# Cross-attention with image prompts on one core: the last batch's sums spread over three engines, its end in chunks of channels, its order written out

## The chip, the cores and the metric

The kernel runs on one core of a Trainium2 chip. The metric is the device time of one launch in microseconds. A core has five engines that each work through their own queue in order: TensorE (PE in the profile; its weight loads are PEld), VectorE (DVE), ScalarE (ACT), GpSimd (POOL) and SyncE (SP, which here only issues DMAs). They wait for each other by semaphores. TensorE reads SBUF and writes PSUM, which here is used as eight banks of 128 x 512 float32.

## The reference

Eight batches; x is 112 x 320 per batch, the context 375 x 512, of which the last 4 rows are image-prompt tokens. There are 20 heads of 16 channels. Everything is float32.

```python
q = heads(hidden_states @ W_q)
k_t = heads(text_ehs @ W_k)
v_t = heads(text_ehs @ W_v)
probs_t = softmax(einsum('bhsd,bhtd->bhst', q, k_t) * attn_scale)
text_out = einsum('bhst,bhtd->bhsd', probs_t, v_t)
...
attn_scores = einsum('bhsd,bhnd->bhsn', q, k_ip) * attn_scale
qsem = _l2norm(einsum('bhst,bte->bhse', probs_t, text_ehs))
sem = einsum('bhse,bne->bhsn', qsem, _l2norm(ip_ehs))
fused = attn_scores + SEM_SCALE * sem
probs_ip = softmax(fused) * spatial_mask[None, None, :, None]
ip_out = einsum('bhsn,bhnd->bhsd', probs_ip, v_ip)
out = (text_out + ip_out) @ W_out + b_out + residual
```

`_l2norm` divides a vector by its length. `qsem` has 512 entries for each head and query, and only its length and its products with four prompt vectors are needed.

## The kernel before

Each batch's 20 heads are treated in five groups of four (`GROUP`, `groups`). For a group:

- `scores` (L467): TensorE multiplies q and k into a PSUM bank `ps_s` of 112 x 371, per head.
- `probabilities` (L485): VectorE takes the negative maximum `nmx` (L489), ScalarE the exponential `p` (L493), and SP sends p to the tile `xg` (L496), without normalisation.
- `transposed` (L500): VectorE transposes `xg` by 32 x 32 blocks into `xgT` (L504).
- `multiplied` (L510): TensorE multiplies p by a wide matrix `u` (L523), 12 blocks of tokens times four heads, into four banks `ps_qd` of up to 392 columns. `u` holds half of the symmetric Gram matrix of the context (so the first 371 columns, multiplied by p and summed, give the squared length of `qsem`), then the products with the prompt vectors, a column of ones (the softmax's sum) and the head's 16 value channels.
- `reduced` (L533): per head, ScalarE copies the last 21 columns to `pvs` (L536), and VectorE multiplies the first 371 columns by p and sums them into one column of `ss` (L538).
- `placed` (L441): GpSimd copies the next group's value channels into `u` (L445), in three pieces, each of which waits until TensorE has read the old ones.

When all heads of a batch are reduced, `finish` (L551) makes the output: roots and reciprocals of `ss` and of the softmax's sum `z`, a softmax over the four prompt logits (L578 to L604), the weighted prompt values `wv` (L606, L612) added to the text part `attn` (L585, L613, L614) on GpSimd or another engine, a transpose on TensorE (L620), its copy `aT` (L624), the output projection `ps_o` (L633), the addition of residual and bias `xb` (L571, L640) and the store (L643). ScalarE loads a table for the root (L579) and another for the exponential (L595).

The loop (L744) runs over batch and group. Scores and probabilities run two groups ahead (`LEAD`), the transpose one ahead. `between` (L665) places pieces of other work after each group: the next batch's Gram matrix, values, keys and context transposes, and one stage of `finish` of the batch before. In the last batch no next batch exists, so only `finish` of batch 6 is there. The last batch's own `finish` comes in two parts: 16 heads (L777, begun after group 3, with its elementwise work on GpSimd), and the last 4 (L782, on VectorE).

Six banks serve the products: four `ps_qd`, two `ps_mm` (function `bank`), and two `ps_sc` hold scores. In the last batch some of the groups' banks come from `ps_mm` (L516).

The order of TensorE, SP and VectorE is as written (L89: `manual_schedule(engines=engines)`). The instructions of ScalarE and GpSimd are ordered by a scheduler from their dependences; only the prologue is written out for all engines.

Of the kernel before, what the change touches and what calls it, by code (L numbers as in the profile page):

```python
# [20 lines left out]
def kernel(  # L21
# [511 lines left out]
    def reduced(b, g):  # L533
        s = st[b]
        for a, (h, ps) in enumerate(zip(groups[g], s.pop(("qd", g)))):
            nc.scalar.copy(s["pvs"][:, h, :], ps[:S, TT:UW])  # L536
            junk = small.tile([S, TT], F32, tag="junk", name=f"junk_{b}_{h}", bufs=1)
            nc.vector.tensor_tensor_reduce(  # L538
                out=junk,
                in0=ps[:S, :TT],  # L540
                in1=s["p", g][:, a, :],
                scale=1.0,
                scalar=0.0,
                op0=ALU.mult,
                op1=ALU.add,
                accum_out=s["ss"][:, h : h + 1],
            )
        del s["p", g]


    def finish(b, heads=(0, H), eng=None, late=False):  # L551

        s = st[b]
        eng = eng or nc.gpsimd
        h0, h1 = heads
        n = h1 - h0
        part = slice(h0, h1)

        def sm(name):
            return small.tile([S, H], F32, tag=name, name=f"{name}_{b}_{h0}", bufs=2)[:, :n]  # L560

        def sm4(name):
            return small.tile([S, H, NIP], F32, tag=name, name=f"{name}_{b}_{h0}", bufs=2)[:, :n]

        def over_ip(t):
            return t.unsqueeze(2).to_broadcast([S, n, NIP])

        pvs = s["pvs"][:, part]
        if not late:
            s["xb"] = work.tile([S, C], F32, tag="xb", name=f"xb_{b}", bufs=1)  # L570
            nc.gpsimd.tensor_tensor(s["xb"], x_sb[:, b, :], bias_sb, ALU.add)  # L571
        z = sm("z")
        nc.vector.tensor_copy(z, pvs[:, :, NIP])

        z2 = sm("z2")
        nc.vector.scalar_tensor_tensor(z2, z, EPS * EPS, z, ALU.mult, ALU.mult)
        rn = sm("rn")
        nc.vector.tensor_tensor(rn, s["ss"][:, part], z2, ALU.max)  # L578
        nc.scalar.activation(rn, rn, AF.Sqrt)  # L579
        nc.vector.reciprocal(rn, rn)  # L580
        zr = sm("zr")
        nc.vector.reciprocal(zr, z)
        attn = attn_ring[b % 2]
        ah = attn[:, :C].rearrange("p (h d) -> p h d", d=D)[:, part]
        eng.tensor_tensor(  # L585
            ah, pvs[:, :, NIP + 1 :], zr.unsqueeze(2).to_broadcast([S, n, D]), ALU.mult
        )
        fu = sm4("fu")
        nc.vector.tensor_tensor(fu, pvs[:, :, :NIP], over_ip(rn), ALU.mult)
        nc.vector.scalar_tensor_tensor(fu, fu, SEM_SCALE, s["ipl"][:, part], ALU.mult, ALU.add)  # L590
        mx = sm("mx")
        nc.vector.tensor_reduce(mx, fu, AX.X, ALU.max)
        nc.vector.tensor_tensor(fu, fu, over_ip(mx), ALU.subtract)
        ex = sm4("ex")
        nc.scalar.activation(ex, fu, AF.Exp)  # L595
        yield

        sx = sm("sx")
        nc.vector.tensor_reduce(sx, ex, AX.X, ALU.add)
        rx = sm("rx")  # L600
        nc.vector.reciprocal(rx, sx)
        nc.vector.tensor_scalar_mul(rx, rx, sm_sb)
        w = sm4("w")
        nc.vector.tensor_tensor(w, ex, over_ip(rx), ALU.mult)  # L604
        wv = work.tile([S, NIP, H, D], F32, tag="wv", name=f"wv_{b}_{h0}", bufs=1)[:, :, :n]
        eng.tensor_tensor(  # L606
            wv,
            s["vip"][:, :, part],
            w.rearrange("p h n -> p n h").unsqueeze(3).to_broadcast([S, NIP, n, D]),
            ALU.mult,  # L610
        )
        eng.tensor_tensor(wv[:, :2], wv[:, :2], wv[:, 2:], ALU.add)  # L612
        eng.tensor_tensor(ah, ah, wv[:, 0], ALU.add)  # L613
        eng.tensor_tensor(ah, ah, wv[:, 1], ALU.add)  # L614
        yield

        i0, i1 = h0 * D // P, -(-h1 * D // P)
        ps = bank(f"ps_a_{b}_{h0}")
        for i in range(i0, i1):
            nc.tensor.transpose(  # L620
                ps[:, i * S : (i + 1) * S], attn[:, i * P : (i + 1) * P], ident[:S, :S]
            )
        aT = work.tile([P, NC, S], F32, tag="aT", name=f"aT_{b}_{h0}")
        nc.scalar.copy(  # L624
            aT[:, i0:i1], ps[:, i0 * S : i1 * S].rearrange("p (i s) -> p i s", s=S)
        )
        yield

        if not late:
# [12 lines left out]

        nc.sync.dma_start(out[b], ob)  # L643
        del st[b]
        yield
# [12 lines left out]
    def run(key, make, pieces=1):  # L658

        if key not in gens:  # L660
            gens[key] = make()
        for _ in range(pieces):
            next(gens[key], None)

    def between(b, g):  # L665

        nb = b + 1
        new = nb < B
        later = [bs for bs in pairs if bs[0] == (nb if b == 0 else nb + 1)]
        if g == 0:  # L670
            if b == 0:
                run(("pp",), None)
            if new:
                run(("g", nb), lambda: gram(nb), 3)
            if b > 0:
                run(("f", b - 1), lambda: finish(b - 1))
        if g == 1:
            if new:
                run(("v", nb), lambda: values(nb), 2)
            run(("t", b), lambda: prompt_logits(b))  # L680
            if b > 0:
                run(("f", b - 1), None)
        if g == 2 and new:
            run(("v", nb), None)
            run(("k", nb), lambda: keys(nb))
        if g == 3:
            if new:
                run(("k", nb), None, 2)
            if b > 0:
                run(("f", b - 1), None)  # L690
        if g == 4:
            if nb + 1 < B:
                run(("c", nb + 1), lambda: transposed_context(nb + 1), 3)
            if b > 0:
                run(("f", b - 1), None)
        if b == 0 and g in (1, 2) or b > 0 and g == 4:
            for bs in later:
                run(("q", bs[0]), lambda: project_queries(bs), 3 if b == 0 else 6)
# [42 lines left out]
    more_constants()  # L741
    prologue.close()

    for n, (b, g) in enumerate(steps):  # L744
        coming = steps[n + LEAD] if n + LEAD < len(steps) else None
        for j, _ in enumerate(multiplied(b, g)):
            at = {0: (0, 1), 4: (2, 3)}.get(j, ())
            for a in at if coming else ():
                scores(*coming, a)
                probabilities(*coming, a)  # L750
            if j == 2 and n + 1 < len(steps):
                transposed(*steps[n + 1])
        reduced(b, g)
        if n + 1 < len(steps):
            placed(*steps[n + 1])
        new = b + 1 < B
        if g == 0 and b > 1:
            run(("f", b - 2), None)
        if new:
            if g == 1:  # L760
                gram_to_dram(b + 1)
                load_next(b + 2)
            elif g == 2:
                gram_to_groups(b + 1, (0, 1))
# [61 lines left out]
```

## Time and profile before

| | |
|---|---|
| median of 3 runs | 498.68 us (497.8 to 499.25) |
| the profiled execution | 498.01 us, span 496.2 us |
| TensorE busy | 468.3 us, 94% of the span |
| VectorE busy | 321.1 us, 65% |
| ScalarE busy | 180.1 us, 36% |
| GpSimd busy | 105.9 us, 21% |
| mean granted clock of TensorE | 0.972 |
| groups 0 to 4 of the last batch, first matmul | 437.13, 445.16, 457.16, 465.80, 471.40 us |
| end of group 4 | 477.05 us |
| last addition `ob` ends | 493.40 us |

All times in the profile are microseconds from the start of the span of one profiled execution; the span is what the engines' records cover, and the execution's own time is 1.81 us more. A line of an engine's order of time gives start, length, engine, line of the kernel, operation and tiles; in square brackets stands how long the engine was idle before it, and what ended that. The slices on the page divide the span into 40; a digit is a busy share in tenths.

### The profile page before, as it was taken

The numbers are of one execution on the slowest core, as the hardware profiler recorded it, in microseconds if no ns is written. First come the engines' busy times: TensorE is split into PE (matmuls) and PEld (weight loads), VectorE is DVE, ScalarE is ACT, GpSimd is POOL, SyncE is SP. The second block draws the span as 40 slices with busy tenths as digits, with TensorE's granted clock in tenths as the row PEclk, the third lists the DMA queues.
The fourth block names the chain that finished last, engine by engine and source line by source line (L and its number), as shares of the span: only waits on it lengthen the run. The fifth ranks groups of instructions, "written<-read, shape, count | busy, mean of one in ns | idle before, by whom it ended". The sixth has DMA issues, their size and how long they took to land.

```text
span 496.2 us, 12853 instructions
## 1 busy us (share of the span) xinstructions
PE 468.3 (94%) x5106; PEld 361.8 (73%) x5106; DVE 321.1 (65%) x692; ACT 180.1 (36%) x505; POOL 105.9 (21%) x245
## 2 busy tenths in 40 slices
PE   6999999999999999999999999999999999987963
PEld 3657777788777787788778787788777887766751
DVE  3045456687765775687756776687756776678862
ACT  2253232235334352335324342335324432243232
POOL 4301200002501124012501124012501232011540
PEclk9997999999999999999999999999999999998895
DMA  7588447542595236942595236842595227732300
GB/s 217 157 198 237 100 152 163 156 114 63 154 228 153 58 95 172 210 121 67 163 229 142 67 98 171 199 116 76 171 220 140 67 87 162 195 101 78 101 13 12
DMA packets 61075, 67.24 MB, mean 136 GB/s; under 512 B 22128, under 2 KB 56192, under 8 KB 61016
## 3 DMA queue, kind: packets, MB, share of 16 engines
q1 hardware_dynamic: 60096, 65.32, 50.3%
q10 hardware_dynamic: 920, 1.11, 0.8%
q8 instruction: 40, 0.66, 0.6%
q14 instruction: 19, 0.16, 0.1%
HBM read 31.65 MB, written 8.17 MB: 80 GB/s over the span
## 4 chain that ended last, share of the span: by engine, by line
PE 84%; DVE 5%; ACT 3%; DMA 2%; POOL 2%; issue 2%; SPq 1%; POOLq 0%; ACTq 0%; DVEq 0%
PE ps_qd L523 37%; PE ps_k L393 11%; PE ps_v L409 11%; PE ps_g L362 9%; PE ps_s L476 7%; PE ps_q L289 2%; PE ps_c L339 2%; PE ps_o L633 2%; DVE junk L538 1%; POOL wv L606 1%; DMA vr<-vd 1%; DVE qm L298 1%; PE ps_kip L237 1%; PE ps_ip L456 1%; DMA ip_sb<-in_ctx_dram 1%
## 5 line engine op out<-in xcount | busy, mean ns | idle before, releaser
L523 PE MATMUL ps_qd<-u,xgT 32*112 32x296 f32 (+11 forms) x3840 | 244.4, 365 | 3.5 <-POOL u L445 1.4
L523 PEld LDWEIGHTS ps_qd<-u,xgT 32*112 32x112 f32 x3840 | 196.8, 174 | 33.6 <-issue 7.3
L493 ACT ACTIVATE p<-ps_s,nmx 112x371 f32<-112x371 f32 x160 | 82.3, 568 | 159.8 <-DVE nmx L489 141.6
L489 DVE TENSOR_REDUCE nmx<-ps_s 112x1 f32<-112x371 f32 x160 | 77.4, 528 | 76.0 <-PE ps_s L476 74.7
L504 DVE STREAM_TRANSPOSE xgT<-xg 128x1536 f32<-128x1536 f32 x40 | 118.9, 2971 | 5.2 <-DMA xg<-p 5.2
L538 DVE CUSTOM_DVE_ANT_0 junk<-ps_qd,p 112x371 f32<-112x371 f32 x160 | 87.1, 544 | 45.3 <-ACT pvs L536 28.0
L476 PE MATMUL ps_s<-kT,qm 32*112 32x371 f32 x320 | 75.0, 496 | 2.8 <-ACT p L493 2.2
L445 POOL COPY u<-vr 128x64 f32<-128x64 f32 x120 | 26.6, 238 | 224.8 <-PE ps_qd L523 161.5
L393 PE MATMUL ps_k<-ctxT,wk_sb 128*128 128x371 f32 x192 | 63.6, 480 | 0.0
L409 PE MATMUL ps_v<-wv_sb,ctxT 128*128 128x320 f32 x192 | 55.6, 440 | 0.0
L393 PEld LDWEIGHTS ps_k<-ctxT,wk_sb 128*128 128x128 f32 x192 | 35.7, 190 | 21.7 <-issue 1.1
L476 PEld LDWEIGHTS ps_s<-kT,qm 32*112 32x112 f32 x320 | 36.8, 173 | 15.8 <-ACT kT L400 3.2
L362 PE MATMUL ps_g<-ctxT 128*128 128x375 f32 (+2 forms) x192 | 45.3, 394 | 0.7 <-issue 0.7
L409 PEld LDWEIGHTS ps_v<-wv_sb,ctxT 128*128 128x128 f32 x192 | 35.2, 190 | 13.5
L362 PEld LDWEIGHTS ps_g<-ctxT 128*128 128x128 f32 x192 | 33.4, 197 | 12.3 <-issue 3.8
L400 ACT COPY kT<-ps_k 128x371 f32<-128x371 f32 x24 | 11.3, 469 | 41.4 <-PE ps_k L393 41.3
L606 POOL TENSOR_TENSOR wv<-vip,w 112x1280 f32<-112x1280 f32 (+1 forms) x8 | 19.2, 2404 | 31.8 <-DVE w L604 31.8
L298 DVE TENSOR_SCALAR qm<-ps_q,emask 128x224 f32<-128x224 f32 (+1 forms) x25 | 9.2, 400 | 24.2 <-PE ps_q L289 24.0
L416 ACT COPY vext<-ps_v 128x320 f32<-128x320 f32 x24 | 10.2, 427 | 33.5 <-PE ps_v L409 33.5
L371 POOL TENSOR_TENSOR ug<-ug,half 128x128 f32<-128x128 f32 (+1 forms) x24 | 11.3, 472 | 41.6 <-ACT ug L370 41.6
L536 ACT COPY pvs<-ps_qd 112x21 f32<-112x21 f32 x160 | 16.5, 200 | 6.9 <-PE ps_qd L523 6.9
L289 PE MATMUL ps_q<-xT,wq_sb 128*128 128x224 f32 (+1 forms) x90 | 16.8, 332 | 1.9 <-ACT xT L284 0.9
(95 smaller groups left out, 272.4 us busy)
## 6 DMA issues: line engine op xcount, KB each, us to landing
xg<-p SPq DMA_DIRECT2D x160, 162.3 KB
u<-ud SPq DMA_DIRECT2D x32, 188.0 KB
vip<-vipd SPq DMA_DIRECT2D x8, 560.0 KB
ct<-in_ctx_dram SPq DMA_DIRECT2D x16, 256.0 KB
u<-ud SPq DMA_DIRECT2D x32, 124.0 KB
vr<-vd SPq DMA_DIRECT2D x32, 120.0 KB
vd<-vext SPq DMA_DIRECT2D x7, 480.0 KB
ud<-ug SPq DMA_DIRECT2D x7, 372.0 KB
```

Of the source, the lines that this page charges most:

```text
L289: nc.tensor.matmul(ps[:, : n * S], wq_sb[:, j, i * P : (i + 1) * P], xT[:, j, : n * S], start=(j == 0), stop=(j == NC - 1),)
L362: nc.tensor.matmul(ps[:, : T - t0], ctxT[:, e, t0 : t0 + P], ctxT[:, e, t0:T], start=(e == 0), stop=(e == NE - 1),)
L393: nc.tensor.matmul(ps[:, :TT], wk_sb[:, e, i * P : (i + 1) * P], s["ctxT"][:, e, :TT], start=(e == 0), stop=(e == NE - 1),)
L409: nc.tensor.matmul(ps[:, :C], ctxT[:, e, c * P : (c + 1) * P], wv_sb[:, e, :], start=(e == 0), stop=(e == NE - 1),)
L445: nc.gpsimd.tensor_copy(region(b, c)[:, :, UV - c * P :], s["vr"][:, c * QN : (c + 1) * QN, g, :])
L476: nc.tensor.matmul(ps[:S, :TT], qm[a * RG : (a + 1) * RG, i, r, j * S : (j + 1) * S], s["kT"][a * RG : (a + 1) * RG, i, :], start=True, st ...
L489: nc.vector.tensor_reduce(nmx, ps[:S, :TT], AX.X, ALU.max, negate=True)
L493: nc.scalar.activation(p, ps[:S, :TT], AF.Exp, bias=nmx)
L504: nc.vector.transpose(xT.rearrange("p j (k q) -> p q j k", q=QN), xg.rearrange("p q (j k) -> p q j k", k=RG),)
L523: nc.tensor.matmul(banks[a][:S, j * RG : UW], xT[a * RG : (a + 1) * RG, j, :S], region(b, c)[a * RG : (a + 1) * RG, q, q * RG :], start=(j ...
L538: nc.vector.tensor_tensor_reduce(out=junk, in0=ps[:S, :TT], in1=s["p", g][:, a, :], scale=1.0, scalar=0.0, op0=ALU.mult, op1=ALU.add, accu ...
L606: eng.tensor_tensor(wv, s["vip"][:, :, part], w.rearrange("p h n -> p n h").unsqueeze(3).to_broadcast([S, NIP, n, D]), ALU.mult,)
```

## The change

1. In `reduced`, for the last batch and all but its last group, heads 1 and 3 of a group no longer use VectorE: ScalarE copies the 371 columns from PSUM to a tile `shared` in SBUF (it takes a buffer of the tag `ctxT`), GpSimd multiplies it by p, and ScalarE runs a copy with an accumulated output to get the sum.
2. In `finish`, for all batches: the copy of `z` is dropped and `pvs` is read in place; `zr` and the first `attn` product move ahead of the root; the multiplication of `rx` by the mask is merged with the product that makes `w`.
3. The last batch's end has three parts by chunks of 128 channels: heads 0 to 7, 8 to 15, and 16 to 19. The first part's two elementwise stages are written within group 3, the second part's after group 3. Tables of ScalarE are preloaded in the last two parts: the exponential's after the root, and the root's after the second part.
4. From group 3 of the last batch on, all engines' order is the written one, ScalarE and GpSimd included.
5. In the last batch `finish` of batch 6 is placed one group earlier in its last two stages, and the load of `vip` (L436) after group 1 instead of group 2.

```diff
@@ reduced
             nc.scalar.copy(s["pvs"][:, h, :], ps[:S, TT:UW])
+            if b == B - 1 and g < NG - 1 and a % 2:
+                if a == 1:
+                    shared = work.tile([P, NE, TP], F32, tag="ctxT", name=f"shared_{b}_{g}")
+                prod = shared[:S, a, :TT]
+                nc.scalar.copy(prod, ps[:S, :TT])
+                nc.gpsimd.tensor_tensor(prod, prod, s["p", g][:, a, :], ALU.mult)
+                nc.scalar.activation(prod, prod, AF.Copy, accum_out=s["ss"][:, h : h + 1])
+                continue
@@ finish
-    def finish(b, heads=(0, H), eng=None, late=False):
+    def finish(b, heads=(0, H), eng=None, written=False):
...
         pvs = s["pvs"][:, part]
-        if not late:
+        z = pvs[:, :, NIP]
+        if h0 == 0:
             s["xb"] = work.tile([S, C], F32, tag="xb", name=f"xb_{b}", bufs=1)
             nc.gpsimd.tensor_tensor(s["xb"], x_sb[:, b, :], bias_sb, ALU.add)
-        z = sm("z")
-        nc.vector.tensor_copy(z, pvs[:, :, NIP])
 
         z2 = sm("z2")
         nc.vector.scalar_tensor_tensor(z2, z, EPS * EPS, z, ALU.mult, ALU.mult)
-        rn = sm("rn")
-        nc.vector.tensor_tensor(rn, s["ss"][:, part], z2, ALU.max)
-        nc.scalar.activation(rn, rn, AF.Sqrt)
-        nc.vector.reciprocal(rn, rn)
         zr = sm("zr")
         nc.vector.reciprocal(zr, z)
...
-        eng.tensor_tensor(
-            ah, pvs[:, :, NIP + 1 :], zr.unsqueeze(2).to_broadcast([S, n, D]), ALU.mult
-        )
+        eng.tensor_tensor(ah, pvs[:, :, NIP + 1 :], over_d(zr), ALU.mult)
+        rn = sm("rn")
+        nc.vector.tensor_tensor(rn, s["ss"][:, part], z2, ALU.max)
+        nc.scalar.activation(rn, rn, AF.Sqrt)
+        if written:
+            nc.scalar.preload_act_table(AF.Exp)
+        nc.vector.reciprocal(rn, rn)
...
-        nc.vector.tensor_scalar_mul(rx, rx, sm_sb)
         w = sm4("w")
-        nc.vector.tensor_tensor(w, ex, over_ip(rx), ALU.mult)
+        nc.vector.scalar_tensor_tensor(w, ex, sm_sb, over_ip(rx), ALU.mult, ALU.mult)
@@ between
+        if g == 2 and not new:
+            run(("f", b - 1), None)
...
-            if b > 0:
+            if b > 0 and new:
                 run(("f", b - 1), None)
@@ the loop
+    parts = [finish(B - 1, (i * HC, (i + 1) * HC), written=i > 0) for i in range(FULL)]
+    tail = ctx.enter_context(ExitStack())
...
+            if j == 6 and n == len(steps) - 2:
+                next(parts[0])
+                next(parts[0])
...
-        if g == 2:
+        if g == (2 if new else 1):
             prompt_values(b)
+        if n == len(steps) - 2:
+            tail.enter_context(tc.manual_schedule())
...
-            first = finish(b, (0, FULL * HC))
-            next(first)
-            next(first)
+            next(parts[1])
+            next(parts[1])
+            nc.scalar.preload_act_table(AF.Sqrt)
     run(("f", B - 2), None)
-    drain(first)
-    drain(finish(B - 1, (FULL * HC, H), nc.vector, late=True))
+    drain(parts[0])
+    last = finish(B - 1, (FULL * HC, H), nc.vector, written=True)
+    next(last)
+    drain(parts[1], last)
```

More of the change, by code (lines that the diff above doesn't have):

```diff
@@ L566, in over_ip, with over_d @@
             return t.unsqueeze(2).to_broadcast([S, n, NIP])
+        def over_d(t):
+            return t.unsqueeze(2).to_broadcast([S, n, D])
         pvs = s["pvs"][:, part]
-        if not late:
+        z = pvs[:, :, NIP]
+        if h0 == 0:
             s["xb"] = work.tile([S, C], F32, tag="xb", name=f"xb_{b}", bufs=1)
             nc.gpsimd.tensor_tensor(s["xb"], x_sb[:, b, :], bias_sb, ALU.add)
-        z = sm("z")
-        nc.vector.tensor_copy(z, pvs[:, :, NIP])
         z2 = sm("z2")
         nc.vector.scalar_tensor_tensor(z2, z, EPS * EPS, z, ALU.mult, ALU.mult)
-        rn = sm("rn")
-        nc.vector.tensor_tensor(rn, s["ss"][:, part], z2, ALU.max)
-        nc.scalar.activation(rn, rn, AF.Sqrt)
-        nc.vector.reciprocal(rn, rn)
         zr = sm("zr")
@@ L627, in finish @@
         yield
-        if not late:
+        if h0 == 0:
             s["o"] = bank(f"ps_o_{b}", spare=b < B - 1)
```

## The prediction

> **What bounds the kernel now.** I read the page first: busy shares, then the slices.
>
> ```profile
> PE 468.3 (94%) x5106; PEld 361.8 (73%) x5106; DVE 321.1 (65%) x692; ACT 180.1 (36%) x505; POOL 105.9 (21%) x245
> ...
> PE   6999999999999999999999999999999999987963
> ...
> PEclk9997999999999999999999999999999999998895
> ```
>
> TensorE fills every slice from the second to the 35th, so the seven earlier batches are set by TensorE. A slice is 12.4 us; in the last five (434 us on) TensorE has holes and its clock dips. All that the edit can win or lose lies there. Next the order of time on each engine from 436 us. TensorE (start, length, operation; in brackets the idle time before it and what ended it):
>
> ```profile
> 445.16 1.27 PE L523 MATMUL ps_qd<-u,xgT 32*112 32x392 f32 x3 [1.04 <-DVE ss L538]
> 451.11 1.42 PE L476 MATMUL ps_s<-kT,qm 32*112 32x371 f32 x2 [2.24 <-ACT p L493]
> 465.80 5.08 PE L523 MATMUL ps_qd<-u,xgT 32*112 32x392 f32 x96 [1.15 <-POOL u L445]
> 471.40 5.77 PE L523 MATMUL ps_qd<-u,xgT 32*112 32x392 f32 x96
> 482.76 0.63 PE L620 MATMUL ps_a<-ident,attn 112*128 112x112 f32 x2 [3.79 <-POOL attn L614]
> ```
>
> These are groups 1, 3 and 4 of the last batch and the first output transpose. ScalarE, same view:
>
> ```profile
> 444.78 1.28 ACT L579 ACT_TABLE_LOAD   x1
> 447.75 0.22 ACT L579 ACTIVATE rn<-rn 112x20 f32<-112x20 f32 x1 [1.69 <-DVE rn L578]
> ...
> 450.48 1.03 ACT L493 ACTIVATE p<-ps_s,nmx 112x371 f32<-112x371 f32 x2 [0.23 <-DVE nmx L489]
> ...
> 483.44 0.35 ACT L624 COPY aT<-ps_a 128x224 f32<-128x224 f32 x1 [5.97 <-PE ps_a L620]
> 483.80 1.28 ACT L579 ACT_TABLE_LOAD   x1
> 485.09 0.20 ACT L579 ACTIVATE rn<-rn 112x4 f32<-112x4 f32 x1
> 486.62 1.28 ACT L595 ACT_TABLE_LOAD   x1 [1.32 <-DVE fu L593]
> ```
>
> The end: group 4 stops at 477.05, GpSimd finishes the 16-head part at 482.71, the queue of ScalarE then runs aT, a table load, a root, a second table load; the last sum (`ob`) ends at 493.40 and the span at 496.2. VectorE and the clock, two more views:
>
> ```profile
> 448.59 0.81 DVE L590 SCALAR_TENSOR_TENSOR fu<-fu,ipl 112x80 f32<-112x80 f32 x1
> 468.27 2.99 DVE L504 STREAM_TRANSPOSE xgT<-xg 128x1536 f32<-128x1536 f32 x1 [0.83 <-DMA xg<-p]
> ```
>
> ```profile
> 453.00:454.00 1.00, 1.00 (x18) 0.98 (x14) 1.00 (x3) 0.00 (x0) 0.00 (x0) 0.50 0.66 187
> 455.00:456.00 1.00, 0.77 (x22) 0.65 (x19) 0.14 (x1) 0.43 (x5) 0.33 (x2) 1.00 0.00 0
> ```
>
> (last three columns: granted clock, DMA share, GB/s.) After the 2.24 us hole TensorE runs at half clock to 454.75.
>
> **What the Trainium skill says.** "ScalarE: Activation LUTs", What ACT_TABLE_LOAD costs: 1283 ns a load, plus a drain of some 1380. The load agrees (1.28); the drain doesn't show, the root starts 0.01 after its load. "TensorE: Matmul & The Clock Gate", Part 1: the clock halves after an idle window of about 3.4 us and returns after a busy one; the half-clock stretch 451.34-454.75 (3.41) agrees, though 2.24 idle sufficed. "GPSIMD Engine Reference", Key points: GpSimd and VectorE share SBUF interfaces when VectorE reads two SBUF inputs. The 0.81 of `fu` above, beside a GpSimd product (448.56-449.30), against 0.19 for the small one at 485.95, fits.
>
> **Prices.** A VectorE sum: 0.695 from one to the next (444.56, 445.25, ...). A copy of 371 columns on ScalarE: 0.47 (row of kT). The ScalarE sum has no row: p of the same size takes 0.57; the same section of the ScalarE page gives 186 ns + 0.833 per element without pointer operands, an estimate of 0.50; bounds 0.41 to 0.75 (a separate read of the accumulator). The GpSimd product, 371 columns: rows 0.47 for 128, 0.86 for 320, 1.55 for 640, so 0.97; bounds 0.72 (the rate of the 1280-wide one, 2.47) to 1.37 (that of the 128-wide).
>
> **The change, walked down the last batch.** The order in which the built program stands decides it, above all on ScalarE and GpSimd.
>
> Group 0's reduction. Before, the root's table load (444.78) lay under VectorE's sums. Now it stands behind copy, GpSimd product, ScalarE sum: first copy done 445.0, products to 446.0 and 447.0, second sum to 447.5, table to 448.8, root to 449.0, against 447.97: +1.05. Behind it VectorE is shorter: `zr` moved out (-0.14), and GpSimd's `attn` now runs at 447.1, not beside `fu` (-0.5). So p of group 3 starts at 450.85 instead of 450.48 and TensorE resumes +0.4 late. Bank release a little earlier (group 1's fourth head now needs 445.1, not 445.8) only lengthens that hole.
>
> Group 1's. VectorE: two sums fewer (-1.39), `rx` multiply gone (-0.28), +0.3 from above: `w` at 458.15, was 459.5. But p of group 4 queues behind the last ScalarE sum: u copies to 456.4, products 456.65 to 458.6, sum to 459.15. p starts 459.2, was 460.05 (-0.85); its last tile ends at 464.15, was 464.70. wv on GpSimd starts 458.67, was 459.59 (-0.9).
>
> Group 2's. The transpose ps_a of batch 6 now stands ahead of group 3 and takes the bank that ScalarE's second copy frees: group end 464.65, four pvs copies and two copies, 465.85. Group 3 starts at 466.25, was 465.80: the hole moves from GpSimd's `u` to this copy.
>
> Group 3 to 4. The read of vip moved on SP ahead of the last four p transfers (its wait is long fulfilled; 560 KB at about 456-459), so these no longer share the queues: landing 2.7 after the last p (as in group 2, where p ends 444.46 and traffic stops at 447.2), 466.85 against 468.27. The VectorE transpose ends 469.85. Then the first 8 heads' chain: z2, zr, rn 0.55; root 0.22; exp table 1.28; exp 0.25; sx, rx, w 0.65: 472.85. GpSimd: 1.08 + 0.69 + 0.46 + 0.46 and gaps 0.28: 475.8. Group 4's `u` copies are queued behind that, so group 4 starts at 476.1, was 471.40: **+4.7**. It ends at 481.3, or 483.0 with one half-clock stretch.
>
> Group 3's sums come after those copies: products to 478.45, sum 479.0, root table 480.3, root, exp table, exp 482.05, and the new preloaded root table 483.35. Only then ScalarE copies group 4's pvs, so group 4's end is covered by 0.35 to 2.
>
> The end. From the first pvs copy to the fourth VectorE sum 2.85 (as at 444.35-447.20): 486.2. z2, zr, attn, rn 0.85: 487.05. Root without a load 0.22, exp load 1.28, exp 0.25: 488.85, where before it was 488.13. From there before needs 5.27 to `ob`; less the `rx` multiply (0.28) 4.99: `ob` ends 493.85, was 493.40. **Sum: +0.45 us.** What the end saves (a root load in the path 1.28, the exp load's wait, no queue behind GpSimd, some 5.9) is what group 4 starts later (4.7) plus the preloaded table (1.3 beyond group 4's likely end).
>
> Hidden edits: in the seven earlier batches `z` copy and `rx` multiply go (0.46 of VectorE each batch) and `attn` moves ahead of two products of the Gram stage on GpSimd; TensorE's own Gram work (5.3 us between groups 0 and 1) covers both. Without that cover they would be worth 3 us.
>
> The sum is made on the profiled execution, 496.2 span and 498.01 whole. +0.45 on the median of 498.68, which lies 0.67 above it, gives **499.1**.
>
> **Rivals.**
> A, slower: the GpSimd product is dear. Four of them are in the path (two in group 0's, two in group 3's). At the upper bound 1.37 they add 4 x 0.40 = 1.6: 500.7. It decides from about 1.24 on (4 x 0.27 makes +1.5). For: small operations on GpSimd cost more per column (472 ns for 128). Against: the rows 320 and 640 bracket 371's rate well.
> B, slower: the hole before group 4 (from the end of ps_o at about 472.8 to 476.1) brings two half-clock stretches: 5.2 + 3.4 = 8.6, end 484.7 instead of 483.35, +1.35 more: 500.5.
> C, faster: before's end hangs on the clock through groups 1 to 3, the new one hardly. If before usually loses one more stretch (1.7) than in its profiled run, as a median 0.67 above it may hint, 499.1 - 1.7 = 497.4, and with a product of 0.8 (4 x 0.17) 496.7.
> D, faster: the chunks pay in full, group 4 ending at 477.05 as before: 477.05 + 2.85 + 0.85 + 1.75 + 4.99 = 487.5, 5.9 less: 492.8. It would need the `u` copies ahead of the wv chain; the built order has them behind.
>
> **How the numbers follow.** Main 0.60, A 0.19, B 0.08, C 0.09, D 0.04. Within 0.3% (1.5 us, about what a measurement of this kernel can tell from no change) is the main case, 0.60; slower A and B, 0.27; faster C and D, 0.13. Its own range is 497.7 to 500.1: product and ScalarE sum within half their bounds, landing 2.3 to 3.0. The range for 8 in 10 leaves out D and the outer ends of A and C: 497.2 to 501.0.
>
> **What would show it.** Right: `u` of group 4 about 476 behind attn on GpSimd; a hole of 3 to 4 us before group 4; a table load just before the last pvs copies; last exp at about 488.6. Wrong: products away from 0.97, a read of the accumulator after each ScalarE sum, group 4 ending later than the preloaded table, p's last transfer landing later than 467.3, or a difference before 436 us.

## The result, and the profile after

| | before | after |
|---|---|---|
| median of 20 runs each | 498.65 us (495.51 to 501.91) | 499.98 us (496.74 to 502.35) |
| ratio of the two | | 1.0032, 95% interval 1.0011 to 1.0052 |
| profiled execution, span | 498.01, 496.2 us | 498.83, 497.0 us |
| mean granted clock in it | 0.972 | 0.975 |

The change costs 1.6 us (0.5 to 2.6): 0.0032 of 498.65. It is just outside what was called "within 0.3%". The forecast was 499.1, with its own range of 497.7 to 500.1. The profiled pair shows only half of the loss, +0.8 in the span, and at a higher clock than before. Where the other half may lie is taken up below.

The page of after, the same three lines:

```profile
PE 467.1 (94%) x5106; PEld 361.1 (73%) x5106; DVE 313.6 (63%) x669; ACT 190.8 (38%) x534; POOL 114.0 (23%) x258
...
PE   5999999999999999999999999999999999996854
...
PEclk9997999999999999999999999999999999998895
```

VectorE has 7.5 us less work, ScalarE 10.7 more, GpSimd 8.1 more. Slices 2 to 35 are as before: the first `p` of the tail, which is the last batch, starts at 439.88 (439.81 before). TensorE from 436 us on, order of time (start, length, operation; in brackets the idle time before and what ended it):

```profile
451.64 1.41 PE L476 MATMUL ps_s<-kT,qm 32*112 32x371 f32 x2 [3.39 <-ACT p L493]
465.39 0.79 PE L631 MATMUL ps_a<-ident,attn 112*128 112x112 f32 x3 [2.08 <-ACT shared L542]
466.11 6.00 PE L523 MATMUL ps_qd<-u,xgT 32*112 32x392 f32 x96
476.95 4.90 PE L523 MATMUL ps_qd<-u,xgT 32*112 32x392 f32 x96 [3.04 <-POOL u L445]
484.81 0.32 PE L631 MATMUL ps_a<-ident,attn 112*128 112x112 f32 x1 [2.96 <-DVE ss L547]
```

The hole before group 3's scores has grown from 2.24 to 3.39; group 4 starts at 476.95 instead of 471.40, behind `u`. ScalarE, same view, groups 0 and 3 and the end:

```profile
446.55 0.19 ACT L544 ACTIVATION_READ_ACCUMULATOR shared<-shared 112x1 f32 x1
...
447.56 1.28 ACT L596 ACT_TABLE_LOAD   x1
448.85 0.22 ACT L596 ACTIVATE rn<-rn 112x20 f32<-112x20 f32 x1
...
479.64 1.28 ACT L596 ACT_TABLE_LOAD   x1
...
482.70 1.28 ACT L800 ACT_TABLE_LOAD   x1
483.99 0.41 ACT L536 COPY pvs<-ps_qd 112x21 f32<-112x21 f32 x4
```

Each ScalarE sum (0.51) is followed by a read of its accumulator (0.19), and each root table now stands behind the sums. Left out between 479.64 and 482.70 are the root, the exponential's table and the exponential. At the end ScalarE is the queue: group 4's matmuls are over at 481.85, and its copies of `pvs` begin at 483.99, behind three table loads. VectorE and GpSimd, two more orders of time:

```profile
467.85 2.94 DVE L504 STREAM_TRANSPOSE xgT<-xg 128x1536 f32<-128x1536 f32 x1 [2.25 <-DMA xg<-p]
```

```profile
476.66 0.59 POOL L445 COPY u<-vr 128x64 f32<-128x64 f32 x3
477.21 1.77 POOL L543 TENSOR_TENSOR shared<-shared,p 112x371 f32<-112x371 f32 x2
```

The copies of `u` and the products of group 3 both wait in GpSimd's queue behind part 0 (the first eight heads), whose last addition runs from 476.26. The last `ob` ends at 494.14 (493.40 before), so the tail is +0.74 in the profiled pair.

**The clock, execution by execution.** The mean granted clock of an execution is not spread evenly: the same kernel shows values near 0.968, 0.972, 0.975, 0.978. In after 10 of 20 executions lie at 0.9705 or below; they average 501.2 us, the other ten 498.6. The profiled one is of the other ten. Of 191 executions of the kernel before, timed along with the experiments, 31 lie there (16%), averaging 500.7; the rest average 498.0. As bookkeeping, then, about 0.9 of the 1.6 us is (0.50 - 0.16) x 2.6, more executions at the low clock, and 0.6 is the rest, 498.6 against 498.0, near to what the profiled pair shows (+0.8). This is an estimate: the line at 0.9705 was drawn after the runs were seen (it falls into a gap of after, between 0.969 and 0.973, but before has 5 executions at 0.970 and 11 at 0.971), and the share of before itself was 8 of 75, 8 of 58 and 15 of 58 in the three series.

### The profile page after: what moved, and what is told of

It is laid out like the page before. It is cut to its first block, busy times and chain, and to the rows that moved or that the text cites. A ratio compares the mean times of both kernels' runs of the same rounds, so it can differ in the third digit from the quotient of the medians.

```text
span 497.0 us, 12880 instructions
## 1 busy us (share of the span) xinstructions
PE 467.1 (94%) x5106; PEld 361.1 (73%) x5106; DVE 313.6 (63%) x669; ACT 190.8 (38%) x534; POOL 114.0 (23%) x258
## 4 chain that ended last, share of the span: by engine, by line
PE 86%; DVE 4%; ACT 4%; DMA 2%; issue 2%; POOL 1%; ACTq 0%; SPq 0%; DVEq 0%
PE ps_qd L523 37%; PE ps_k L393 12%; PE ps_v L409 11%; PE ps_g L362 9%; PE ps_s L476 7%; PE ps_q L289 2%; PE ps_o L644 2%; PE ps_c L339 2%; DVE xgT L504 2%; DMA xg<-p 1%; DMA ct<-in_ctx_dram 1%; PE ps_kip L237 1%; DVE qm L298 1%; PE ps_ip L456 1%; POOL shared L543 1%
## 5 line engine op out<-in xcount | busy, mean ns | idle before, releaser
L523 PE MATMUL ps_qd<-u,xgT 32*112 32x104 f32 (+11 forms) x3840 | 242.6, 364 | 4.4 <-POOL u L445 3.0
L547 DVE CUSTOM_DVE_ANT_0 junk<-ps_qd,p 112x371 f32<-112x371 f32 x152 | 82.8, 544 | 44.6 <-ACT pvs L536 28.5
L416 ACT COPY vext<-ps_v 128x320 f32<-128x320 f32 x24 | 10.2, 426 | 33.5 <-PE ps_v L409 33.5
L644 PE MATMUL ps_o<-wo_sb,aT 128*112 128x320 f32 x48 | 16.7, 480 | 3.4 <-ACT aT L635 2.9
L339 PE MATMUL ps_c<-ident,ct 128*128 128x128 f32 (+1 forms) x96 | 13.9, 293 | 4.5 <-DMA ct<-in_ctx_dram 3.9
```

The source lines that it names most:

```text
L523: nc.tensor.matmul(banks[a][:S, j * RG : UW], xT[a * RG : (a + 1) * RG, j, :S], region(b, c)[a * RG : (a + 1) * RG, q, q * RG :], start=(j ...
L547: nc.vector.tensor_tensor_reduce(out=junk, in0=ps[:S, :TT], in1=s["p", g][:, a, :], scale=1.0, scalar=0.0, op0=ALU.mult, op1=ALU.add, accu ...
L644: nc.tensor.matmul(ps[:S, :C], aT[:, i, :], wo_sb[:, i, :], start=(i == 0), stop=(i == NC - 1))
```

## The experiments

Times are turned into microseconds against the kernel before with its 498.4 us. "Low" counts the executions at a clock of 0.9705 or below.

| run | what stands | ratio, 95% interval | us | low |
|---|---|---|---|---|
| after | the change | 1.0032 (1.0011 to 1.0052) | +1.6 | 10 of 20 |
| e3 | the same order on every engine | 1.0040 (1.0019 to 1.0060) | +2.0 | 13 of 22 |
| e5 | `vip` after group 2 | 1.0030 (1.0008 to 1.0051) | +1.5 | 13 of 22 |
| e13 | batch 6's stages where they were | 1.0064 (1.0039 to 1.0088) | +3.2 | 7 of 11 |
| e4 | no preloaded root table | 1.0038 (1.0014 to 1.0062) | +1.9 | 12 of 19 |
| e7 | `u` first, written order | 1.0059 (1.0041 to 1.0078) | +2.9 | 13 of 18 |
| e6 | group 3's sums on VectorE | 1.0017 (0.9993 to 1.0042) | +0.8 | 10 of 22 |
| e2 | before, with the split alone | 1.0015 (0.9997 to 1.0033) | +0.7 | 19 of 22 |
| e11 | group 0's sums on VectorE | 0.9999 (0.9977 to 1.0020) | 0.0 | 1 of 14 |
| e1 | all sums on VectorE | 0.9956 (0.9938 to 0.9974) | -2.2 | 1 of 22 |
| e9 | e1, `u` first | 0.9949 (0.9933 to 0.9966) | -2.5 | 0 of 22 |
| e10 | e9, no preloaded root table | 0.9939 (0.9915 to 0.9963) | -3.0 | 0 of 17 |
| e12 | e10, ps_a after group 3 | 0.9973 (0.9948 to 0.9998) | -1.3 | 2 of 19 |

The runs are named by the number they begin with. Edits are shown against the changed kernel, except that e2 is shown against the kernel before, e10 against e9 and e12 against e10. The theory to begin with: the end by chunks is a gain, the split of the sums spends it, by putting the sums into ScalarE's queue ahead of root tables and group 4's `pvs`. The rival: group 4's late start (behind `u` on GpSimd) is the loss, whatever the sums do. Each interval reaches about 1 us to either side, so a difference between two runs of under about 1.5 us is not told from none.

### The split undone, and the split alone

```diff
@@ reduced
-            if b == B - 1 and g < NG - 1 and a % 2:
+            if b == B and a % 2:
```

`b == B` is never true, so no sum is split.

> The changed kernel with all 16 sums of groups 0 to 3 of the last batch back on VectorE; the rest of the change stays. Theory (the split costs, the end by chunks gains): VectorE can end group 3's four sums at 476.3 (four of 0.70 from 473.54) instead of ScalarE at 479.62, root and Exp of part 1 end 2 us earlier, the preloaded root table is in ScalarE by 479.6, group 4's copies of pvs follow its last matmul (481.85) at once instead of at 483.99, so -2.1 there, and group 0's root comes 0.4 earlier. Sum about -2.4 against the changed kernel, 0.8 to 1.0 faster than the kernel before (ratio 0.998). Rival (the lateness of group 4's matmuls alone sets the end, the split is harmless): no difference from the changed kernel, ratio 1.002 to 1.004.

Measured: 0.9956, 3.8 us better than after. The theory's sign holds and the rival falls: group 4's matmuls still start behind `u`, about as late as in after, and the time is gained all the same. TensorE and ScalarE of this run at the end:

```profile
477.07 4.80 PE L523 MATMUL ps_qd<-u,xgT 32*112 32x392 f32 x96 [0.59 <-POOL u L445]
```

```profile
478.98 0.21 ACT L596 ACTIVATE rn<-rn 112x8 f32<-112x8 f32 x1 [2.56 <-DVE rn L595]
...
480.75 1.28 ACT L800 ACT_TABLE_LOAD   x1
482.04 0.41 ACT L536 COPY pvs<-ps_qd 112x21 f32<-112x21 f32 x4
```

The root follows VectorE's sums at 478.98 instead of 480.93, as its table is loaded under them, and `pvs` follows at 482.04 instead of 483.99: 1.95 earlier, where 2.1 was expected. But the whole gain was expected at 2.4 and came out at 3.8. The clock would account for most of the surplus: 1 of 22 executions is low instead of half of them, and (0.50 - 0.05) x 2.6 is 1.2, an estimate at the price that a low execution has in after.

```diff
@@ reduced
             nc.scalar.copy(s["pvs"][:, h, :], ps[:S, TT:UW])
+            if b == B - 1 and g < NG - 1 and a % 2:
...
+                continue
```

> The kernel before with the split of the sums alone. Theory: +0.4 to +0.5 at group 0 (root table behind ScalarE's second sum), +0.7 at group 3 (the second ScalarE sum ends at about 473.6, then 1.28 of root table, root at 475.0 where it was 474.26, and GpSimd's wv chain of 16 heads, which ends last before the end, moves with it); sum +0.8 to +1.3, ratio 1.002 to 1.003. Rival (the split is a gain by itself, VectorE being freed of two sums of 0.70 in each group): -0.5 to -1, ratio 0.998 to 0.999.

The lines left out are those of the change: copy to `shared`, product on GpSimd, sum on ScalarE. Measured: +0.7, interval -0.1 to +1.6. It leans to the theory, does not tell the loss from none, and excludes the rival's gain (-0.5 to -1). Its low share is the highest of all, 19 of 22, and its hole before group 3's scores the longest:

```profile
452.77 1.42 PE L476 MATMUL ps_s<-kT,qm 32*112 32x371 f32 x2 [3.89 <-ACT p L493]
```

Yet its low executions average 499.1 and its other three 498.4, 0.7 apart and not 2.6. So the price of a low execution in after does not hold for every kernel.

### Group 0's sums alone

```diff
@@ reduced
-            if b == B - 1 and g < NG - 1 and a % 2:
+            if b == B - 1 and 0 < g < NG - 1 and a % 2:
```

> The changed kernel with group 0's sums alone back on VectorE (groups 1 to 3 stay split). Theory (part of the loss is group 0's: root table behind ScalarE's second sum, TensorE's hole before group 3's scores 3.39 us instead of 1.60 with the sums on VectorE): TensorE resumes at about 450.95 instead of 451.64 and, with a shorter hole, spends no more time at half clock: -0.7 to -1.5 against the changed kernel, ratio to the kernel before 1.000 to 1.0015. Rival (group 3's ScalarE chain takes all of the loss, and what group 0 saves waits there): 0 to -0.3, ratio 1.003.

Measured: 0.9999, 1.65 us better than after, somewhat more than the theory gave; the rival's 1.003 lies outside the interval, though this interval and that of after overlap a little. TensorE of this run:

```profile
451.13 1.02 PE L476 MATMUL ps_s<-kT,qm 32*112 32x371 f32 x3 [1.59 <-ACT p L493]
```

Counted from the first `p` of the tail (440.50 here, 439.88 in after), TensorE resumes 10.63 us later instead of 11.76, so 1.13 is saved at the hole; 0.9 of it is left when group 4 starts (476.66). And the low executions go from 10 of 20 to 1 of 14 (e7, timed beside it with group 0's sums split, has 13 of 18). This run differs from after in group 0's sums only, so the low executions are shown to hang on them. That they do so through the length of the hole is not shown apart from this, but over all kernels the share goes with it:

| hole before group 3's scores | kernels | low |
|---|---|---|
| 1.6 us (group 0's sums on VectorE) | e1, e9, e10, e11, e12 | 4 of 94 |
| 2.24 us | before | 31 of 191 |
| 3.38 to 3.39 us | after, e3, e4, e5, e6, e7, e13 | 78 of 134 |
| 3.89 us | e2 | 19 of 22 |

Each hole is read in one profiled execution. The last row hangs on where the line is drawn: at 0.9695 it would be 8 of 22, while the others would be 1 of 94, 26 of 191 and 76 of 134.

What a low execution is can be seen where the profiled one is low. The windows view of after and then of e4 (no preloaded root table), behind that hole; each row gives a stretch, its length, the busy time of TensorE, its weight loads, VectorE, ScalarE and GpSimd, then the granted clock, DMA share and GB/s:

```profile
455.00:456.00 1.00, 1.00 (x34) 1.00 (x29) 0.00 (x0) 0.61 (x2) 0.24 (x1) 1.00 0.06 16
```

```profile
455.00:459.00 4.00, 3.59 (x40) 3.40 (x39) 2.02 (x7) 1.88 (x9) 2.21 (x4) 0.50 0.59 182
...
464.00:465.00 1.00, 1.00 (x18) 0.89 (x14) 1.00 (x1) 0.00 (x0) 0.92 (x2) 0.72 0.63 169
```

By the same view, microsecond by microsecond, the clock is at half from 451.5 to 454.9 in after (3.4) and from 450.9 to 464.6 in e4 (13.7, four times as long), though TensorE is 100% busy by this view in each microsecond from 458 to 464. Group 1 and most of group 2 then run at half speed. The profiled executions of e2 and e7, low ones too, show 13.7, that of e13 10.2, those of e5 and e6, which are not low, 3.4. (Later stretches of 6.8 stand in e1, e4, e9 and e10. So, the stretch that runs to the end left out, the lengths seen are one, two, three and four times 3.41.) That the low executions without a profile are of this kind is inferred from their clock. The Trainium skill, "TensorE: Matmul & The Clock Gate", Part 1, says that the window which decides is free-running and its length about 3.4 us, so that one kernel's executions differ by its phase. The spread between executions agrees with that; that the clock stays down for 13.7 us, six of them without a break in TensorE's work, does not fit the one busy window after which it is to return, and why it does so is open.

### The copies of u first, and group 3's sums

```diff
@@ the loop
                 next(parts[0])
-                next(parts[0])
+        if n == len(steps) - 2:
+            placed(*steps[n + 1])
+            next(parts[0])
         reduced(b, g)
```

Left out, here and in e6, e7 and e9: the call of `placed` behind `reduced` is skipped at this step, as it now stands ahead.

> The changed kernel with one thing moved: GpSimd's three copies of u for group 4 stand ahead of part 0's product wv instead of behind its last addition. Group 4's matmuls then start at about 473.0 instead of 476.95 and end at about 478. Theory (group 3's products on GpSimd, still behind part 0's additions, and the ScalarE chain behind them set the end): the products move by the 0.55 of the copies only, group 4's copies of pvs still come at 483.4, and the time is 0.3 to 0.6 below the changed kernel, ratio to the kernel before 1.002. Rival (the late start of group 4 sets the end): -3.5 to -4, ratio 0.995.

Measured: 1.0040. It tests neither: at that place the scheduler still orders GpSimd, and it put the copies back behind part 0, so that the order is that of after. GpSimd of this run:

```profile
476.91 0.45 POOL L625 TENSOR_TENSOR attn<-attn,wv 112x128 f32<-112x128 f32 x1
477.30 0.58 POOL L445 COPY u<-vr 128x64 f32<-128x64 f32 x3
```

It is a repeat of after, and shows how well a repeat agrees: 2.0 against 1.6.

With the same edit, and group 3's sums on VectorE:

```diff
@@ reduced
-            if b == B - 1 and g < NG - 1 and a % 2:
+            if b == B - 1 and g < NG - 2 and a % 2:
```

> As the run with the copies of u first, and group 3's sums (only these) all on VectorE. Theory (two holds one behind the other: the late start of group 4, and ScalarE's queue with group 3's sums and the preloaded root table): both are gone, group 4 ends at about 478, ScalarE has the root table by 480.4 and the copies of pvs follow, where they stood at 483.99: -3.4 to -3.8 against the changed kernel, ratio to the kernel before 0.995 to 0.997. Rival (either hold is enough of itself, or group 0 to 2 lose what shows): -0.5 to -2.4 only.

Again the copies did not move, so this is after with group 3's sums on VectorE. Measured: +0.8, 0.75 better than after, within the uncertainty of none, where -3.4 to -3.8 was expected of an edit that would have moved `u` too; its span in the profile is 495.2, 1.8 better. Now ScalarE has its root table by 481.0 and waits for TensorE:

```profile
482.22 0.41 ACT L536 COPY pvs<-ps_qd 112x21 f32<-112x21 f32 x4 [1.21 <-PE ps_qd L523]
```

So the two holds stand one behind the other: with the ScalarE chain shortened, group 4's late start (477.40 here) becomes the one that ends last. In this trace, taking away the first is worth the difference, not its full length. (E11 and e6 together undo the split in groups 0 and 3 and gain 2.4 of e1's 3.8; groups 1 and 2 were not tried alone.)

To move the copies in fact, the written order has to begin one step earlier:

```diff
@@ the loop
                 next(parts[0])
-                next(parts[0])
+        if n == len(steps) - 2:
+            tail.enter_context(tc.manual_schedule())
+            placed(*steps[n + 1])
+            next(parts[0])
         reduced(b, g)
```

Left out, here and in e9: the old place of `manual_schedule`, behind `prompt_values`, is empty.

> The changed kernel with the written order beginning one step earlier, so that GpSimd's three copies of u for group 4 really stand ahead of part 0's wv (in the earlier run with that aim the planner put them back behind it). Group 4's matmuls then start at about 473.5 to 474.3, when the last matmul of batch 6's output projection ends, instead of 476.95. Theory (the chain of group 3's products on GpSimd, still behind part 0's additions at 477.2, sums on ScalarE, three table loads, then the copies of pvs, sets the end): 0 to -0.6 against the changed kernel, ratio to the kernel before 1.002 to 1.003. Rival (the late start of group 4 sets the end): -2.5 to -3.5, ratio 0.996 to 0.998.

Measured: 1.0059, worse than after by 1.3 and than its repeat e3 by 0.9, which the intervals hardly tell from none, and far from the rival's gain. TensorE and ScalarE of this run:

```profile
474.22 6.40 PE L523 MATMUL ps_qd<-u,xgT 32*112 32x392 f32 x96
487.29 0.42 PE L631 MATMUL ps_a<-ident,attn 112*128 112x112 f32 x1 [6.66 <-DVE ss L547]
```

```profile
479.33 0.51 ACT L544 ACTIVATE shared<-shared 112x371 f32<-112x371 f32 x1 [4.32 <-POOL shared L543]
...
479.84 0.24 ACT L536 COPY pvs<-ps_qd 112x21 f32<-112x21 f32 x2
```

Group 4 starts 2.7 earlier by the clock of the trace (1.6 counted from the first `p` of the tail, 438.76 here), and gains nothing: its matmuls end at 480.62, and its `pvs` comes at 486.38. The edit brought a new wait, too: as written, ScalarE sums the group's second head (waiting 4.32 for GpSimd) before it copies the third and fourth, an order that the scheduler had avoided. And this profiled execution is a low one. So the run speaks against the rival where the sums are split, as group 4's matmuls are done 5.8 before their results are fetched, but it is no clean measure of the theory.

### vip, batch 6's stages, the preloaded table

```diff
@@ the loop
-        if g == (2 if new else 1):
+        if g == 2:
             prompt_values(b)
```

> The changed kernel with the load of vip issued after group 2 again, behind the last two transfers of p. The forecast held that these transfers land 2.7 us after the end of the last p once vip no longer shares the queues; the profile showed 3.6 (transpose at 467.85, p's end 464.25), as before the change. Theory now (the landing is 3.6 by itself, vip has no part in it): the transpose of group 4 starts 3.5 to 3.7 after p's end, time within 0.3 us of the changed kernel. Rival (vip does compete, something else made up the difference): 4.3 to 4.6 after p's end, +0.7 to +1.0.

Measured: 1.0030, no difference from after. VectorE of this run:

```profile
467.91 2.94 DVE L504 STREAM_TRANSPOSE xgT<-xg 128x1536 f32<-128x1536 f32 x1 [2.33 <-DMA xg<-p]
```

The last `p` ends at 464.23 here, so the transpose starts 3.68 behind it; in after 3.60, in before 3.57. `vip` has no part in it.

```diff
@@ between
-        if g == 2 and not new:
-            run(("f", b - 1), None)
...
-            if b > 0 and new:
+            if b > 0:
                 run(("f", b - 1), None)
```

> The changed kernel with batch 6's ps_a, output projection and last addition where they stood before the change (ps_a after group 3, the other two after group 4); all else as changed. Theory (moving them one group earlier paid nothing, as p's landing, GpSimd's order and the ScalarE chain set what follows): group 3's matmuls begin 0.6 to 0.9 earlier, group 4's stay at 476.9 behind u, VectorE has the addition of 0.49 ahead of the last z: 0 to +0.5 against the changed kernel, ratio to the kernel before 1.003 to 1.0045. Rival (the hole before ps_a cost half clock in group 3): -0.5 to -2, ratio 0.999 to 1.002.

Measured: 1.0064, 1.6 worse than after and 1.7 worse than e5, timed beside it (the theory gave at most 0.5), and the rival has the wrong sign. So the move seems to have been worth something, though the intervals overlap. The cause is only partly seen: `ob` of batch 6 stands in the last VectorE chain (490.00, ahead of `z`), and the hole before group 4 is 7.20 with nothing between, where after has `ps_o` in it; half clock then lasts from 475 to 485 in the profiled execution. With 11 executions, 7 of them low, more can't be said.

```diff
@@ the loop
             next(parts[1])
             next(parts[1])
-            nc.scalar.preload_act_table(AF.Sqrt)
```

> The changed kernel without the preloaded root table ahead of group 4's copies of pvs (1.28 us, 482.70 to 483.98); the table is then loaded behind the copies of pvs and aT. Theory: group 4's matmuls end at 481.85 and ScalarE is free at 482.7, so the copies of pvs and the four sums behind them move up by the whole 1.28, and the table (to about 485.5 to 486.7) ends 0 to 1 us after rn is ready: -0.6 to -1.2 against the changed kernel, ratio to the kernel before 1.001 to 1.002. Rival (the preload is a gain, as it takes the table out of the last chain): +0.3 to +1.3, ratio 1.004 to 1.006.

Measured: 1.0038, 0.3 worse than after, uncertain by more than 1; the run decides for neither case. Its profiled execution is a low one, in which TensorE, not the table, holds `pvs`:

```profile
487.10 0.41 ACT L536 COPY pvs<-ps_qd 112x21 f32<-112x21 f32 x4 [1.77 <-PE ps_qd L523]
...
488.54 1.28 ACT L596 ACT_TABLE_LOAD   x1
490.48 0.21 ACT L596 ACTIVATE rn<-rn 112x4 f32<-112x4 f32 x1 [0.66 <-DVE rn L595]
```

Group 4 came so late there that ScalarE was free, so taking the table away paid nothing in this execution; nor did it cost, as it is loaded 0.66 before `rn` comes. The theory's 1.28 needs group 4 to be early, and that was read from an execution at the higher clock.

### A version that beats both

All sums on VectorE, and `u` first with the written order from there:

```diff
@@ reduced
-            if b == B - 1 and g < NG - 1 and a % 2:
+            if b == B and a % 2:
@@ the loop
-                next(parts[0])
+        if n == len(steps) - 2:
+            tail.enter_context(tc.manual_schedule())
+            placed(*steps[n + 1])
+            next(parts[0])
```

> The same written order with u first, and all sums on VectorE (the split undone as in the first run of this study). Theory: group 4 ends about 2 us earlier than in that run, but its copies of pvs stand in ScalarE's queue behind group 3's root, two Exp steps and the preloaded root table (482.04 there), and those start from group 3's matmuls, which do not move: 0 to -0.6 against that run, ratio to the kernel before 0.994 to 0.996. Rival (with the ScalarE chain shortened, group 4's matmuls are what ends last): -2, ratio 0.991.

Measured: 0.9949, 0.35 better than e1, where the theory had 0 to 0.6; the intervals don't tell it from none. Group 4 starts at 476.46 behind `ps_o`, 0.6 earlier. Then, less the preloaded table:

```diff
@@ the loop
-            nc.scalar.preload_act_table(AF.Sqrt)
```

> The run with u first and all sums on VectorE, less the preloaded root table for group 4. The table is then loaded in its place behind the copies of pvs and of aT, where ScalarE waits for rn anyway. Theory: the copies of pvs move up by 1.28, the end by 0.8 to 1.3 against that run. Rival (the table comes in behind the wait and costs what it saved): 0 to +1.3.

Measured: 0.9939, **3.0 us (1.8 to 4.2) faster than the kernel before**, 4.6 faster than the change, the best of the study. Against e9 it is 0.5, which the intervals don't tell from none. ScalarE of this run shows that the copies of `pvs` no longer wait for the table, but for TensorE:

```profile
479.35 0.41 ACT L536 COPY pvs<-ps_qd 112x21 f32<-112x21 f32 x4 [0.49 <-PE ps_qd L523]
```

Last, batch 6's `ps_a` back behind group 3, and its projection and addition in the last chain:

```diff
@@ between, and the end
-        if g == 2 and not new:
-            run(("f", b - 1), None)
...
-    run(("f", B - 2), None)
     drain(parts[0])
...
     next(last)
+    run(("f", B - 2), None, 2)
     drain(parts[1], last)
```

> The run without the preload (u first, all sums on VectorE) with batch 6's transposition ps_a back behind group 3's matmuls, and its output projection and last addition behind ScalarE's root table of the last chain. TensorE then has no wait for group 2's sums (bank) before group 3's matmuls. Theory (that wait, 3.1 us of hole with u, and the half clock that follows it, 7.25 us for 96 matmuls that take 4.8 at full clock, are the largest loss left): group 3 ends 2 to 3 us earlier, group 4 starts 2 us earlier, -1.5 to -3 against that run, ratio to the kernel before 0.988 to 0.991. Rival (the landing of p and the transpose of group 4 at 467.9 to 470.9 hold part 0 and group 4 anyway, and the clock falls as before): 0 to -0.5, ratio 0.993.

Measured: 0.9973, 1.7 worse than e10, about as much as the two intervals leave open, and far from the gain of 1.5 to 3 that was expected: a miss. TensorE of e10 and then of this run:

```profile
464.83 0.79 PE L631 MATMUL ps_a<-ident,attn 112*128 112x112 f32 x3 [3.18 <-DVE ss L547]
465.55 7.25 PE L523 MATMUL ps_qd<-u,xgT 32*112 32x392 f32 x96
```

```profile
463.00 5.25 PE L523 MATMUL ps_qd<-u,xgT 32*112 32x392 f32 x96 [0.94 <-POOL u L445]
...
471.13 7.82 PE L523 MATMUL ps_qd<-u,xgT 32*112 32x392 f32 x94 [0.96 <-ACT aT L635]
```

Group 3 does gain its 2 us (5.25 against 7.25), and group 4 gives it back: two matmuls in (at 470.2), it waits for the copy of `aT`, and then runs 94 matmuls in 7.82 with part of them at half clock. This profiled execution is the shortest span of all (491.8), at a clock of 0.984, yet the runs reach from 493.6 to 501.4. Why they average worse than e10's stays open.

## Why the prediction was nearly right, and where its sizes were off

Its steps against the profile of after, in microseconds from the span's start:

| step | forecast | measured |
|---|---|---|
| `p` of group 3; TensorE resumes | 450.85; 451.5 | 451.01; 451.64 |
| wv of batch 6 on GpSimd | 458.67 | 458.67 |
| last `p` of group 4 ends | 464.15 | 464.25 |
| group 3's first matmul | 466.25 | 466.11 |
| transpose of group 4 starts | 466.85 | **467.85** |
| group 4 starts; ends | 476.1; 481.3 | 476.95; 481.85 |
| group 3's last ScalarE sum ends | 479.0 | 479.62 |
| preloaded table ends | 483.35 | 483.98 |
| fourth sum of group 4 | 486.2 | 486.84 |
| last exponential ends | 488.85 | 489.12 |
| `ob` ends (before 493.40) | 493.85 | 494.14 |

**The mechanism held.** Earlier batches unchanged, the end's saving spent on group 4's later start and on ScalarE's queue, the preloaded table ending beyond group 4: all are in the trace. E1 shows from the other side that the rest of the change, the end by chunks above all, is worth 2.2 us against the kernel before once the split is taken out. But part of the closeness is luck: 499.98 lies only 0.12 inside its own range, the loss of 1.6 is more than three times the 0.45 forecast, and the end came within 0.3 only because errors of opposite sign cancelled. Two of the prediction's own signs of being wrong also showed: a read of the accumulator after each ScalarE sum, and a late landing of `p`.

**The step that failed: "so these no longer share the queues: landing 2.7 after the last p".** It is 3.60, and e5 shows that taking `vip` out of the way changed nothing. The 2.7 was the end of the traffic behind group 2's `p`, not the start of the instruction that waits. The windows view of after, the last two numbers being DMA share and GB/s:

```profile
467.00:468.00 1.00, 1.00 (x12) 0.56 (x8) 0.15 (x1) 0.98 (x4) 0.00 (x0) 0.50 0.08 24
468.00:469.00 1.00, 1.00 (x16) 0.55 (x12) 1.00 (x1) 1.00 (x1) 0.00 (x0) 0.70 0.00 0
```

Traffic goes on past 467, and the transpose starts at 467.85, behind the last packet. The error of 1.0 shrank to 0.6 at ScalarE's sums and 0.3 at the end, since other terms were priced too dear: the pair of GpSimd products took 1.77 (1.94 assumed), and the chain from the fourth sum to the last exponential 2.28 (2.65).

**The term that was missing.** The longer hole before group 3's scores was priced as time alone, +0.4, and that was right (+0.46). A price in clock was left out. Rival C asked whether the kernel before often loses one more stretch than in its profile; it is the changed kernel that more often has the low clock, and by the estimate above about 0.9 of the 1.6 goes with that. The sum of one profiled execution against another could not show it.

**Small terms.** The ScalarE sum: 0.51 and the read of the accumulator, 0.61 from start to end, where 0.50 was taken and 0.75 allowed for. The root table started behind the sums as the order said (447.56). `fu` beside no GpSimd product: 0.24, was 0.81; but `w` now lies beside one and takes 0.62. The seven other batches show no gain from the dropped copy and multiplication, as said.

**Readings and sums.** The `fu` at 485.95 takes 0.17, not 0.19. 487.05 and 1.75 make 488.80, not 488.85. The 4.7 and 1.3 that close the sum make 6.0, where the shift of `pvs` by its own figures is 483.35 - 477.05 = 6.3. The first two move the forecast by 0.05 at most, the third is only its summary. And the kernel before has a second half-clock stretch that the prediction passes over, 458.4 to 461.8, in group 2; in after the second one is from 465.4 to 468.8, in group 3.

**The rivals.** A (product dear, from 1.24 on): 0.84 to 0.98, out. B (two half-clock stretches in group 4): not in this profile; group 4 runs at full clock, 4.90. But the profiled executions of e4 and e13 show 7.5 for it, with half clock for 6.8 and 10.2 around it, so something like it happens in kernels close to this one. C is out as put. D (the chunks paid in full) needed `u` ahead of wv; e9 and e10 have it, and with the sums back on VectorE gain 2.5 and 3.0 of the 5.9.

## What to carry to other kernels

Before moving sums off a busy engine, look at the queue that takes them: here two ScalarE sums a group went ahead of a root table, the table lost its cover, and the next stage stood in the same queue. A hole on TensorE may cost twice, by its length and by the chance of half clock that goes with it; here one profiled execution told the first only, so compare the granted clocks of all runs before trusting a difference between two profiles. And where two holds stand one behind the other, undo them together, and look at the built order to see that an edit moved anything at all.

## What the runs showed of the hardware that was not expected

- After a hole the half-clock stretch has more than one length: 3.4 us in the profiled execution of after, 13.7 in that of e4, after the same hole of 3.38 to 3.39. Over the profiled executions the stretches, but for the one that runs to the end, are 3.4, 6.8, 10.2 or 13.7 long, as if the clock were decided anew every 3.41 us.
- The share of low executions goes with the hole over these kernels: 4 of 94 at 1.6 us, 31 of 191 at 2.24, 78 of 134 at 3.39; e2's 19 of 22 at 3.89 depends on the line drawn.
- A ScalarE copy with an accumulated output is followed by a separate read of the accumulator, 0.19 us.
- From the end of a producer to the start of the VectorE instruction that waits for its SBUF-to-SBUF transfer pass 3.5 to 3.7 us (3.57 in before, 3.60 in after, 3.68 in e5), with or without a load of 560 KB issued right behind it; in e13 it is 4.06.
- A table load takes 1.28 us in every profiled execution, which is the 1283 ns of the Trainium skill ("ScalarE: Activation LUTs", What ACT_TABLE_LOAD costs). The drain of some 1380 ns that the same section adds shows in none: where the next instruction has its operands, it starts 0.01 to 0.02 after the load (447.56 + 1.28, then 448.85).
